# Moving work across the stage boundaries of a two-layer graph kernel: adjacency sums, scaling of h, last stores

## The chip, the cores and the metric

The kernel runs on one NeuronCore of a Trainium2 chip. The metric is the device time of one execution in microseconds (us), taken as the median of several runs. Five engines work side by side: PE (matmul), DVE (VectorE), ACT (ScalarE), POOL (GpSimd) and SP (issues DMAs). Each runs its own instructions in order.

## The reference

Two layers work on `x`, 16 batches of 1024 nodes with 256 channels, all in float32, with an adjacency matrix `adj` of 1024x1024.

- Layer 0: a graph gate (column means, sigmoid of differences, product with `adj`) gives queries, `x @ kv_w` gives keys and values, four heads of attention follow, and `x1 = layernorm(x + attention)`.
- Layer 1: `A_hat` is `adj + I`, scaled by the inverse roots of its degrees on both sides. Then

```
agg = A_hat @ x1                      # per batch
h   = relu(batchnorm(agg @ W1.T + b1))   # statistics over all batches and nodes, 512 channels
o   = batchnorm(h @ W2.T + b2)           # again over all batches and nodes, 256 channels
out = layernorm(x1 + o)
```

Each batch norm needs its statistics over all 16 batches before any of its outputs can be scaled, so it cuts the kernel into stages.

## The kernel before, in words

`fast_path` does the work (a second path is taken only when the softmax denominators leave a safe range). It has four stages. In all of them the order of the instructions on PE, ACT and DVE is the order in which the Python code issues them (`tc.manual_schedule`). The order on POOL and SP is chosen by the framework's scheduler. The framework also adds all waits: a tile's buffer is reused when its readers are done, and a pool of tiles that is laid over a closed pool waits for all of that pool's readers.

1. **Attention** (batches 0 to 15, `scores` L895 and `outputs` L911, in bursts of two units). The hooks `normalise` (L940: denominators into a PSUM tile, copy, DMAs to turn them), `residual` (L964: transposes of the outputs into PSUM, multiplication on DVE, addition to x on POOL) and `finish_x1` (L981: layer norm with eight `bn_stats` and eight scalings on DVE, then the store of x1 to DRAM on POOL's queue) are due some bursts after their group. In the last batch the adjacency is transposed, gets its degrees and is scaled: `scale_adjacency(m)` (L1070, one DVE instruction for each of eight row blocks `aht[m]`).
   After the last burst (L1197 to L1207), the aggregation of batch 0 runs as plain matmuls over m (`aggregate_first`, L1092) into two PSUM tiles of 1024 columns (`tile_s`), with one `scale_adjacency` ahead of each m. The last `normalise` and the last two `residual` stand at m=1 and m=4. Two ACT copies of 1024 columns take the sums out. Then follow on DVE the 16 additions of `adjacency_sums` (L1075) and the last `finish_x1`.
2. **Aggregation and first linear** (L1233 to L1411). Batches 1 to 15 use seven products in place of eight (`products`, L604: p1, p6, p2, p7, p5, p4, p3), of sums made beforehand: `x1_sums` on POOL for each batch, `adjacency_sums` once, `right_sums` (tile tT, DVE) for the linear. The aggregation of batch b and the linear of batch b−1 alternate on PE: after each of the seven aggregation steps `run_linear(lin, 2)` runs two linear steps (L1371 to L1375). Each step's product is added or copied by DVE or ACT, in turn on three PSUM banks a, b and c; a product that accumulates on a bank waits until the step before has read it. The h of each batch goes to DRAM. The last batch's linear (L1393 to L1411) is plain, with the batch norm's coefficients (`coefficients1`: one `bn_aggr` on DVE, five small POOL instructions) behind each of four k.
3. **Second linear** (L1420 to L1476). h is loaded in pieces of 2 MB into pool `hl` (two buffers), scaled by ACT (`scale_shift1`, L1386, four activations per batch) one batch ahead, and multiplied (L1457): for each of two output blocks c, four k and two halves. DVE takes the result out (L1468) and makes its statistics (L1472). `o2p` holds the output of all 16 batches. `hl` is opened after it.
4. **Residual and layer norm** (L1483 to L1588). `scale_shift` on ACT, transposes on PE with x1 added, statistics on DVE, ten small POOL instructions for the coefficients (among them a power, L1556), then `finish` (L1561): two blocks of 256 columns on DVE, six on ACT, and one store of 1 MB on SP's queue. x1 is loaded into `xp` (three buffers) and pool `fin2` (four).

Of the kernel before, what the change touches and what calls it, by code (L numbers as in the profile page):

```python
# [515 lines left out]
def fast_path(  # L516
# [74 lines left out]
    def layernorm(t, name):  # L591
# [7 lines left out]
        for n in range(NCH):  # L599
            nc.vector.tensor_scalar(  # L600
                t[:, n, :], t[:, n, :], mv[:, n, 0:1], rstd[:, n : n + 1], ALU.subtract, ALU.mult
            )

    def products(name, bank, out, mm, temps, bias):  # L604

# [94 lines left out]
    with (  # L700
# [391 lines left out]
        def aggregate_first(m):  # L1092
            if m == 0:
                agg[0] = xTp.tile([P, CC, N], F32, tag="xT", name="agg_0")
                agg["ps"] = [tile_s(f"pagg_{c}") for c in range(CC)]
            for c in range(CC):
                for hs in (H0, H1):
                    nc.tensor.matmul(
                        agg["ps"][c][:, hs], x1l[0][:, m, c * P : (c + 1) * P], aht[m][:, hs],
                        start=(m == 0), stop=(m == NCH - 1),  # L1100
                    )
            if m == NCH - 1:
                for c in range(CC):
                    nc.scalar.copy(agg[0][:, c, :], agg["ps"][c])

# [10 lines left out]
        with tc.manual_schedule(engines={mybir.EngineType.PE, mybir.EngineType.Activation, mybir.EngineType.DVE}):  # L1116
# [116 lines left out]
    with (  # L1233
# [126 lines left out]
        for b in range(1, B):  # L1360
            if b + 1 < B:
                load_x1l(b + 1)
                x1_sums(b + 1)
            else:
                h0 = []
# [27 lines left out]
        for k in range(HC):  # L1393
            ps = [bank(f"ph_{k}_{half}") for half in range(2)]
            for c in range(CC):
                for half, hs in enumerate((H0, H1)):
                    nc.tensor.matmul(  # L1397
                        ps[half], w1T[:, c, k * P : (k + 1) * P], t[:, c, hs],
                        start=(c == 0), stop=(c == CC - 1),
                    )  # L1400
            if k == HC - 1:
                scale_shift1(h0[0], 0)
            for half, hs in enumerate((H0, H1)):
# [4 lines left out]
            coefficients1(k)  # L1408
        for k in range(1, HC):
            scale_shift1(h0[k], k)  # L1410
# [8 lines left out]

    with tc.tile_pool(name="o2p", bufs=1) as o2p:  # L1420
        o2T = [
# [9 lines left out]
        coefficients2, sg2, sh2 = batchnorm(bn2_st, cols["g2"], cols["be2"], CC, "bn2")  # L1431
        with (
            tc.tile_pool(name="hl", bufs=2) as hl,
            tc.manual_schedule(
                engines={mybir.EngineType.PE, mybir.EngineType.Activation, mybir.EngineType.DVE}
            ),
        ):
# [8 lines left out]
            for b in range(B):  # L1446
                if b + 2 < B:
                    load_h(b + 2)
                if b + 1 < B:
                    for k in range(HC):  # L1450
                        scale_shift1(hs_of[b + 1][k], k)
                h = hs_of.pop(b)
                for c in range(CC):
                    ps = tile_s(f"po2_{b}_{c}")
                    for k in range(HC):
                        for hs in (H0, H1):
                            nc.tensor.matmul(  # L1457
                                ps[:, hs], w2T[:, k, c * P : (c + 1) * P], h[k][:, hs],
                                start=(k == 0), stop=(k == HC - 1),
                            )  # L1460
                    if b == B - 1 and c == CC - 1:
                        for hs in (H0, H1):
# [21 lines left out]
        with (  # L1484
            tc.tile_pool(name="fin2", bufs=4) as fin2,
            tc.tile_pool(name="ps_held", bufs=3, space=PSUM) as ps_held,
# [4 lines left out]
        ):  # L1491
            for b in range(3, 7):
                load_x1(b, fin2, "xf")

# [18 lines left out]

            def residual2(b):
                xt = xf[b]
# [39 lines left out]
                pool.tensor_tensor(var, var, dif, ALU.add)  # L1555
                pool.tensor_tensor(rstd, var, mhalf, ALU.pow)  # L1556
                pool.tensor_tensor(nmr, nmr, rstd, ALU.mult)
# [3 lines left out]
            def finish(b, rstd, nmr):  # L1561
                xt, hx = xf.pop(b), held.pop(b)
                y = o2T[b].rearrange("p c n -> p (c n)").rearrange("p (n c) -> p n c", c=C)
                for n in (0, 1):
                    nc.vector.tensor_scalar(
                        y[:, n, :], xt[:, n, :], rstd[:, n : n + 1], nmr[:, n : n + 1],
                        ALU.mult, ALU.add,
                    )
                for n in (4, 5, 6, 7, 2, 3):
                    nc.scalar.activation(  # L1570
                        y[:, n, :], hx[:, (n - 4) * C : (n - 3) * C] if n >= 4 else xt[:, n, :],
                        AF.Identity, bias=nmr[:, n : n + 1], scale=rstd[:, n : n + 1],
                    )
                nc.sync.dma_start(out[b].rearrange("(n p) c -> p n c", p=P), y)
                if b + 7 < B:
                    load_x1(b + 7, *((fin2, "xf") if 3 <= b < 7 else (xp, "x")))

# [4 lines left out]
            for b in range(B):  # L1582
                coeffs[b] = residual2(b)
                if b + 1 < B:
                    scale_shift(b + 1)
                if b:
                    finish(b - 1, *coeffs.pop(b - 1))
            finish(B - 1, *coeffs.pop(B - 1))  # L1588


# [41 lines left out]
```

## Time and profile before

| | us |
|---|---|
| median of 3 runs | 2637.98 (2637.81 to 2638.22) |
| the profiled execution's own time | 2637.64 |
| its span, first to last instruction | 2635.9 |
| its mean granted PE clock | 0.996 |
| stage boundary 1 to 2 | near 1708 to 1800 |
| stage boundary 2 to 3 | near 2294 to 2330 |
| last instruction that computes, its end | 2628.7 |

The profile gives for each engine the time in which it was busy, and ahead of each instruction the idle time with what ended it ("<-"). A 128x512 float32 matmul appears as two records. The end of a matmul is modelled, so the distance from start to start is the safer measure. A line number names the line of the kernel. Names are those of the program's tiles: `a_agg`, `b_agg`, `c_agg` the three banks of the aggregation's products, `a_h`, `b_h`, `c_h` those of the linear, `po` the second linear, `hl` loaded h, `hw` written h, `u_h` a temporary of the linear.

### The profile page before, as it was taken

What the parts mean: (1) busy time and instruction counts of PE and PEld (TensorE: products, weight loads), DVE (VectorE), ACT (ScalarE), POOL (GpSimd) and SP (SyncE); (2) the same over time, 40 slices, a digit from 0 to 9 for tenths busy, and PEclk for the clock granted to TensorE, in tenths of its full rate; (3) what the DMA queues carried; (4) which work ended last, traced back from release to release, by engine and by line L of the source; (5) the groups of instructions that cost most, each with busy time, mean ns of one, the idle gap of its engine ahead of it and who ended that gap; (6) DMA issues with size and microseconds to landing.
All of it is one profiled execution on the core that took longest, in us unless ns stands there. A gap on an engine that the chain in (4) does not pass through costs nothing. (4 is left out here: it accounts for less than half of the span.)

```text
span 2635.9 us, 32325 instructions
## 1 busy us (share of the span) xinstructions
PE 2572.7 (98%) x13158; PEld 1118.6 (42%) x13158; DVE 1587.8 (60%) x2159; ACT 1110.2 (42%) x1321; POOL 338.9 (13%) x407
## 2 busy tenths in 40 slices
PE   8999999999999999999999999999999999999986
PEld 4443444444434444444344443334444444444455
DVE  5465665756656657566566576766565565533367
ACT  5363563644635636546356364501100111133358
POOL 0001000100000001001000010232221122000036
PEclk9999999999999999999999999999999999999999
DMA  4001101011011010110110110112222222254458
GB/s 144 2 9 41 33 10 41 17 25 33 9 41 33 10 41 19 23 33 9 41 33 9 41 49 2 41 55 89 96 76 84 86 90 96 96 201 150 159 194 303
DMA packets 134557, 168.96 MB, mean 64 GB/s; under 512 B 86784, under 2 KB 120064, under 8 KB 124032
## 3 DMA queue, kind: packets, MB, share of 16 engines
q1 hardware_dynamic: 129568, 116.47, 14.1%
q0 software_dynamic: 4832, 50.34, 4.6%
q8 instruction: 105, 1.72, 0.3%
q14 instruction: 52, 0.43, 0.0%
HBM read 99.36 MB, written 67.44 MB: 63 GB/s over the span
## 5 line engine op out<-in xcount | busy, mean ns | idle before, releaser
L908 ACT ACTIVATE p<-ps 128x1024 f32<-128x1024 f32 x512 | 495.6, 1020 | 179.7 <-PE ps L903 132.6
L933 DVE TENSOR_TENSOR acc<-acc,p 128x1024 f32<-128x1024 f32 x384 | 483.2, 1258 | 60.9 <-ACT p L908 32.3
L903 PE MATMUL ps<-qT,kT 64*64 64x512 f32 x4096 | 490.5, 594 | 1.4 <-ACT p L908 1.4
L924 PE MATMUL po<-p,v 64*64 64x512 f32 x4096 | 485.3, 589 | 0.0
L805 PE MATMUL pg<-wg,x 128*128 128x512 f32 x960 | 425.2, 596 | 0.0
L979 POOL TENSOR_TENSOR x<-x,o 128x512 f32<-128x512 f32 x64 | 109.5, 1711 | 1434.8 <-DVE o L974 1434.8
L924 PEld LDWEIGHTS po<-p,v 64*64 64x64 f32 x4096 | 156.7, 133 | 282.8 <-issue 282.6
L805 PEld LDWEIGHTS pg<-wg,x 128*128 128x128 f32 x960 | 177.6, 190 | 226.9 <-issue 203.3
L903 PEld LDWEIGHTS ps<-qT,kT 64*64 64x64 f32 x4096 | 146.1, 132 | 280.2 <-issue 231.5
L817 ACT ACTIVATE qT<-qT 128x512 f32<-128x512 f32 x64 | 40.1, 630 | 481.9 <-DVE qT L814 481.9
L1457 PE MATMUL po<-hl,w12T 128*128 128x512 f32 x512 | 222.0, 596 | 3.6 <-ACT hl L1387 2.8
L814 DVE SCALAR_TENSOR_TENSOR qT<-pg,para_s 128x512 f32<-128x512 f32 x64 | 43.9, 689 | 270.7 <-PE pg L805 269.8
L793 DVE SCALAR_TENSOR_TENSOR wg<-wg,adj_s 128x1024 f32<-128x1024 f32 x128 | 153.1, 1217 | 16.0 <-ACT wg L789 16.0
L1457 PEld LDWEIGHTS po<-hl,w12T 128*128 128x128 f32 x512 | 97.7, 191 | 127.9 <-issue 120.4
L784 ACT ACTIVATE wg<-crow,ccol 128x1024 f32<-128x1024 f32 x128 | 146.6, 1146 | 12.2 <-DMA crow<-c 12.2
L789 ACT ACTIVATE wg<-wg 128x1024 f32<-128x1024 f32 x128 | 135.5, 1059 | 2.6
L1387 ACT ACTIVATE hl<-hl,bn_sh,bn_sg 128x1024 f32<-128x1024 f32 x64 | 74.4, 1229 | 137.4 <-DMA hl<-h 136.1
L855 PE MATMUL pv<-kvw_s,xT 128*128 128x256 f32 x512 | 124.0, 385 | 1.6 <-ACT kT L846 1.6
L1468 DVE TENSOR_SCALAR o<-po,col_b 128x1024 f32<-128x1024 f32 x31 | 39.8, 1283 | 138.1 <-PE po L1457 138.1
L842 PE MATMUL pk<-xT,kvw_s 128*128 128x512 f32 x256 | 120.3, 592 | 0.0
L855 PEld LDWEIGHTS pv<-kvw_s,xT 128*128 128x128 f32 x512 | 94.9, 190 | 51.9 <-issue 27.6
L1286 PE MATMUL b_agg<-aT,x1S 128*128 128x512 f32 x240 | 109.2, 598 | 0.0
(159 smaller groups left out, 2641.4 us busy)
## 6 DMA issues: line engine op xcount, KB each, us to landing
h<-hw POOLq DMA_DIRECT2D x16, 2048.0 KB, 6.6
hl<-h SPq DMA_DIRECT2D x15, 2048.0 KB
x<-x POOLq DMA_DIRECT2D x16, 1024.0 KB, 4.2
x1l<-x SPq DMA_DIRECT2D x16, 1024.0 KB
xf<-x SPq DMA_DIRECT2D x16, 1024.0 KB
out_dram<-o SPq DMA_DIRECT2D x16, 1024.0 KB
x<-in_x_dram SPq DMA_DIRECT2D x15, 1024.0 KB
crow<-c SPq DMA_DIRECT2D x15, 512.0 KB
```

What stands on the lines that cost most here:

```text
L784: nc.scalar.activation(w, s["crow"], AF.Abs, bias=s["ccol"][:, n : n + 1])
L789: nc.scalar.activation(w, w, AF.Tanh, scale=0.5)
L793: nc.vector.scalar_tensor_tensor(w, w, 1.0, adj_s[:, n, :], op0=ALU.subtract, op1=ALU.mult)
L805: nc.tensor.matmul(ps, xt[:, n, c * P : (c + 1) * P], s["wg", n][:, hs], start=(n == 0), stop=(n == NCH - 1),)
L842: nc.tensor.matmul(ps, kvw_s[:, c, kc * P : (kc + 1) * P], s["xT"][:, c, hs], start=(c == 0), stop=(c == CC - 1),)
L855: nc.tensor.matmul(pt[:, j * C : (j + 1) * C], s["xT"][:, c, n * P : (n + 1) * P], kvw_s[:, c, C : 2 * C], start=(c == 0), stop=(c == CC - 1),
L903: nc.tensor.matmul(ps[kh * D : (kh + 1) * D, hd * HALF : (hd + 1) * HALF], kT[r, pr, ks], qT[r, pr, qh * HALF : (qh + 1) * HALF], start=Tr ...
L908: nc.scalar.activation(p, ps, AF.Exp)
L924: nc.tensor.matmul(g["po"][kh][hd * D : (hd + 1) * D, :], s["v"][r, m, h * D : (h + 1) * D], p[r, hd * HALF : (hd + 1) * HALF], start=(m = ...
L933: nc.vector.tensor_add(g["acc"], g["acc"], p)
L979: nc.gpsimd.tensor_tensor(xs, xs, o.rearrange("p n h d -> p n (h d)"), ALU.add)
L1457: nc.tensor.matmul(ps[:, hs], w2T[:, k, c * P : (c + 1) * P], h[k][:, hs], start=(k == 0), stop=(k == HC - 1),)
```

## The change

It has these parts:

- **PSUM of the first boundary.** The sums of `aggregate_first` go to four tiles of 512 columns (the two `tile_o` and the two `tile_t`), in the order c = 1, 0, with four copies of 512 columns. The last `den` and the last two `poT` use `tile_s`.
- **Order of DVE there.** All seven remaining `scale_adjacency` stand ahead of m = 0, the `adjacency_sums` at m = 1 to 4, ahead of the last residuals. `finish_x1(15)` becomes `layernorm_steps`: statistics on DVE (and two more small POOL instructions) at the end of the loop, the scaling as eight ACT activations behind the first aggregation step of batch 1, followed by the store of x1, the load of `x1l(2)` and `x1_sums(2)`. In batch 1 the linear's steps start one aggregation step later and come in threes at i = 3 and 5.
- **Last linear of stage 2.** The halves are the outer loop of the matmuls. `scale_shift1(h0[k-2])` stands behind `coefficients1(k)`.
- **Stage 3.** Pool `hl` is opened ahead of `o2p` and lives on through stage 4. Batch 0 does k = 0, 1 for both c, then k = 2, 3. The last block of batch 15 does one half after the other. Both PSUM tiles of a batch are declared ahead of its matmuls.
- **Stage 4.** x1 of batches 3 to 6 and 10 to 13 is loaded in pairs into the buffers of `hl`; `fin2` is gone. For the last batch, the small coefficient instructions move from POOL to DVE (the power stays), `finish(14)` stands ahead of them, DVE does four blocks and ACT four, and the store is split into two halves, one on SP's queue and one on ACT's.

```diff
+    def layernorm_steps(t, name):
...
+        def statistics():
+            for n in range(NCH):
+                nc.vector.bn_stats(st[:, n, :], t[:, n, :])
+                nc.vector.bn_aggr(mv[:, n, :], st[:, n, :])
+            rsqrt(rstd, mv[:, :, 1], EPS)
+            nc.gpsimd.tensor_tensor(nmr, mv[:, :, 0], rstd, ALU.mult)
+            nc.gpsimd.tensor_scalar(nmr, nmr, -1.0, None, ALU.mult)
+
+        def apply():
+            for n in range(NCH):
+                nc.scalar.activation(
+                    t[:, n, :], t[:, n, :], AF.Identity,
+                    bias=nmr[:, n : n + 1], scale=rstd[:, n : n + 1],
+                )
...
-            den = tile_t(f"den_{k}")
+            last = k == B * PAIRS - 1
+            den = tile_s("den_last")[:, H0] if last else tile_t(f"den_{k}")
...
-            pt = tile_t(f"poT_{k}")
+            if (b, pr) == (B - 1, PAIRS - 1):
+                pt = tile_s(f"poT_{k}")[:, H0]
+            else:
+                pt = tile_t(f"poT_{k}")
...
-                agg["ps"] = [tile_s(f"pagg_{c}") for c in range(CC)]
-            for c in range(CC):
-                for hs in (H0, H1):
+                agg["ps"] = [[tile(f"pagg_{i}") for i in range(2)] for tile in (tile_o, tile_t)]
+            for c in (1, 0):
+                for half, hs in enumerate((H0, H1)):
...
             if m == NCH - 1:
-                for c in range(CC):
-                    nc.scalar.copy(agg[0][:, c, :], agg["ps"][c])
+                for c in (1, 0):
+                    for half, hs in enumerate((H0, H1)):
+                        nc.scalar.copy(agg[0][:, c, hs], agg["ps"][c][half])
...
             for m in range(NCH):
-                if m + 1 < NCH:
-                    scale_adjacency(m + 1)
+                if m == 0:
+                    for k in range(1, NCH):
+                        scale_adjacency(k)
+                elif m < 4:
+                    adjacency_sums(m - 1)
+                elif m == 4:
+                    adjacency_sums(3)
                 aggregate_first(m)
                 run(sums.get(j + m - 1, []), 9)
                 run(full.get(j + m, []), 9)
-            for i in range(NCH // 2):
-                adjacency_sums(i)
-            run(late.get(j + 5, []), 9)
+            x_last = st.pop(B - 1)["x"]
+            last_statistics, last_apply = layernorm_steps(x_last, f"l0_{B - 1}")
+            last_statistics()
...
-                run_linear(lin, 2)
+                if b > 1 or i > 0:
+                    run_linear(lin, 3 if b == 1 and i in (3, 5) else 2)
+                if b == 1 and i == 0:
+                    last_apply()
+                    nc.gpsimd.dma_start(x1_d[B - 1], x_last)
+                    load_x1l(2)
+                    x1_sums(2)
...
-            for c in range(CC):
-                for half, hs in enumerate((H0, H1)):
+            for half, hs in enumerate((H0, H1)):
+                for c in range(CC):
...
-            if k == HC - 1:
-                scale_shift1(h0[0], 0)
...
             coefficients1(k)
-        for k in range(1, HC):
+            if k > 1:
+                scale_shift1(h0[k - 2], k - 2)
+        for k in range(2, HC):
             scale_shift1(h0[k], k)
...
-    with tc.tile_pool(name="o2p", bufs=1) as o2p:
+    with tc.tile_pool(name="hl", bufs=2) as hl, tc.tile_pool(name="o2p", bufs=1) as o2p:
...
+                pss = [tile_s(f"po2_{b}_{c}") for c in range(CC)]
...
+                if b == 0:
+                    for ks in (range(HC // 2), range(HC // 2, HC)):
+                        for c in range(CC):
+                            for k in ks:
+                                for hs in (H0, H1):
+                                    mm(c, k, hs)
...
+                    if b:
+                        for k, hs in (
+                            [(k, hs) for hs in (H0, H1) for k in range(HC)] if last
+                            else [(k, hs) for k in range(HC) for hs in (H0, H1)]
+                        ):
+                            mm(c, k, hs)
...
-            for b in range(3, 7):
-                load_x1(b, fin2, "xf")
...
+            load_x1_pair(3)
+            load_x1_pair(5)
...
+                if b == B - 1:
+                    between()
...
-                pool = nc.gpsimd
+                pool = nc.vector if b == B - 1 else nc.gpsimd
...
-                pool.tensor_tensor(rstd, var, mhalf, ALU.pow)
+                nc.gpsimd.tensor_tensor(rstd, var, mhalf, ALU.pow)
...
-                for n in (0, 1):
+                last = b == B - 1
+                for n in (0, 1, 2, 3) if last else (0, 1):
...
-                for n in (4, 5, 6, 7, 2, 3):
+                for n in (4, 5, 6, 7) if last else (4, 5, 6, 7, 2, 3):
...
+                if last:
+                    nc.sync.dma_start(dst[:, M0, :], y[:, M0, :])
+                    nc.scalar.dma_start(dst[:, M1, :], y[:, M1, :])
+                else:
+                    nc.sync.dma_start(dst, y)
+                if b in (4, 6):
+                    load_x1_pair(b + 6)
```

More of the change, by code (lines that the diff above doesn't have):

```diff
@@ L602, in layernorm @@
             )
+    def layernorm_steps(t, name):
+        st = small.tile([P, NCH, 6], F32, tag="ln_st", name=f"st_{name}")
+        mv = small.tile([P, NCH, 2], F32, tag="ln_mv", name=f"mv_{name}")
+        rstd = small.tile([P, NCH], F32, tag="ln_rs", name=f"rs_{name}")
+        nmr = small.tile([P, NCH], F32, tag="ccol", name=f"nm_{name}")
+        def statistics():
[11 more added lines that the diff above has]
+                )
+        return statistics, apply
     def products(name, bank, out, mm, temps, bias):
@@ L1094, in aggregate_first @@
                 agg[0] = xTp.tile([P, CC, N], F32, tag="xT", name="agg_0")
-                agg["ps"] = [tile_s(f"pagg_{c}") for c in range(CC)]
-            for c in range(CC):
-                for hs in (H0, H1):
+                agg["ps"] = [[tile(f"pagg_{i}") for i in range(2)] for tile in (tile_o, tile_t)]
+            for c in (1, 0):
+                for half, hs in enumerate((H0, H1)):
                     nc.tensor.matmul(
-                        agg["ps"][c][:, hs], x1l[0][:, m, c * P : (c + 1) * P], aht[m][:, hs],
+                        agg["ps"][c][half], x1l[0][:, m, c * P : (c + 1) * P], aht[m][:, hs],
                         start=(m == 0), stop=(m == NCH - 1),
@@ L1360, in fast_path @@
         for b in range(1, B):
-            if b + 1 < B:
+            if 1 < b < B - 1:
                 load_x1l(b + 1)
                 x1_sums(b + 1)
-            else:
+            elif b == B - 1:
                 h0 = []
@@ L1431, in fast_path @@
         coefficients2, sg2, sh2 = batchnorm(bn2_st, cols["g2"], cols["be2"], CC, "bn2")
[L1432 to L1436, printed above, removed]
+        with tc.manual_schedule(
+            engines={mybir.EngineType.PE, mybir.EngineType.Activation, mybir.EngineType.DVE}
         ):
@@ L1452, in fast_path, with mm @@
                 h = hs_of.pop(b)
-                for c in range(CC):
[L1454 to L1461, printed above, removed]
+                pss = [tile_s(f"po2_{b}_{c}") for c in range(CC)]
+                def mm(c, k, hs):
+                    nc.tensor.matmul(
+                        pss[c][:, hs], w2T[:, k, c * P : (c + 1) * P], h[k][:, hs],
+                        start=(k == 0), stop=(k == HC - 1),
+                    )
+                if b == 0:
[4 more added lines that the diff above has]
+                                    mm(c, k, hs)
+                for c in range(CC):
+                    ps = pss[c]
+                    last = b == B - 1 and c == CC - 1
+                    if b:
[5 more added lines that the diff above has]
+                    if last:
                         for hs in (H0, H1):
@@ L1484, in fast_path @@
         with (
-            tc.tile_pool(name="fin2", bufs=4) as fin2,
             tc.tile_pool(name="ps_held", bufs=3, space=PSUM) as ps_held,
@@ L1491, in fast_path, with load_x1_pair @@
         ):
-            for b in range(3, 7):
-                load_x1(b, fin2, "xf")
+            pairs = {}
+            def load_x1_pair(b):
+                pairs[b] = hl.tile([P, 2, NCH, C], F32, tag="hl", name=f"xf_{b}_{b + 1}")
+                for i in range(2):
+                    xf[b + i] = pairs[b][:, i]
+                    nc.sync.dma_start(xf[b + i], x1_d[b + i])
+            load_x1_pair(3)
+            load_x1_pair(5)
             def scale_shift(b):
@@ L1512, in add_x1, with residual2 @@
                 )
-            def residual2(b):
+            def residual2(b, between):
                 xt = xf[b]
@@ L1573, in finish @@
                     )
-                nc.sync.dma_start(out[b].rearrange("(n p) c -> p n c", p=P), y)
-                if b + 7 < B:
-                    load_x1(b + 7, *((fin2, "xf") if 3 <= b < 7 else (xp, "x")))
+                dst = out[b].rearrange("(n p) c -> p n c", p=P)
+                if last:
+                    nc.sync.dma_start(dst[:, M0, :], y[:, M0, :])
[4 more added lines that the diff above has]
+                    load_x1_pair(b + 6)
+                elif b + 7 < B and not 3 <= b < 7:
+                    load_x1(b + 7, xp, "x")
             add_x1(0, 2)
@@ L1582, in fast_path, with before @@
             for b in range(B):
-                coeffs[b] = residual2(b)
+                def before(b=b):
+                    if b:
+                        finish(b - 1, *coeffs.pop(b - 1))
+                coeffs[b] = residual2(b, before)
                 if b + 1 < B:
                     scale_shift(b + 1)
-                if b:
-                    finish(b - 1, *coeffs.pop(b - 1))
+                    before()
             finish(B - 1, *coeffs.pop(B - 1))
```

## The prediction

> **What bounds the kernel now.** I first read the page's busy times, then PE's list of waits, then timeline and clock around each wait, and last the chain at the end.
>
> ```profile
> PE 2572.7 (98%) x13158; PEld 1118.6 (42%) x13158; DVE 1587.8 (60%) x2159; ACT 1110.2 (42%) x1321; POOL 338.9 (13%) x407
> ```
>
> PE is 98% busy, and the diff removes no matmul. A gain can only come from PE's 63 us of idle time, from time in which PE ran slowly, and from the tail after PE's last matmul. The waits of PE that lie where the diff edits:
>
> ```profile
> PE b_h L1318 <- DVE u_h L615: 3.4, 2, 1.9
> PE po L1457 <- ACT hl L1387: 2.8, 1, 2.8
> PE b_h L1318 <- DVE tT L667: 1.8, 1, 1.8
> PE a_agg L1286 <- ACT agg L1104: 1.1, 1, 1.1
> ```
>
> (total us, times, longest.) PE's timeline at the first boundary, attention to aggregation:
>
> ```profile
> 1741.21 3.70 PE L1286 MATMUL a_agg<-ahT,x1l 128*128 128x512 f32 x8 [1.10 <-ACT agg L1104]
> 1744.75 1.02 PE L1318 MATMUL a_h<-agg,w12T 128*128 128x512 f32 x2
> 1747.54 1.10 PE L1318 MATMUL b_h<-tT,wS 128*128 128x512 f32 x2 [1.77 <-DVE tT L667]
> ...
> 1757.06 1.02 PE L1318 MATMUL c_h<-tT,wS 128*128 128x512 f32 x2
> 1759.95 1.57 PE L1318 MATMUL b_h<-tT,w12T 128*128 128x512 f32 x2 [1.88 <-DVE u_h L615]
> 1761.31 4.90 PE L1286 MATMUL b_agg<-aT,x1S 128*128 128x512 f32 x8
> 1766.05 1.02 PE L1318 MATMUL c_h<-agg,wS 128*128 128x512 f32 x2
> ```
>
> Undisturbed, two records take 0.86 us from start to start and eight take 3.43. At 1761.31 eight take 4.74: the granted clock halves after the 1.88 us wait. (Columns: window and length, busy us of PE, PEld, DVE, ACT and POOL, granted clock, DMA share, GB/s.)
>
> ```profile
> 1761.00:1762.00 1.00, 1.00 (x2) 0.34 (x1) 0.44 (x1) 0.00 (x0) 0.00 (x0) 0.50 1.04 434
> 2328.00:2329.00 1.00, 1.00 (x2) 0.34 (x1) 0.00 (x0) 1.00 (x2) 0.00 (x0) 0.50 0.97 401
> ```
>
> The second line is the other boundary, first linear to second. The chain of waits there:
>
> ```profile
> 2309.47 6.63 DMA h<-hw
> ...
> 2316.25 8.34 DMA hl<-h
> ...
> 2324.69 1.25 ACT hl L1387
> ```
>
> The load of h(1) starts only when the last store of h has landed; then its scaling, then PE.
>
> **First boundary.** Costs by starts of PE instructions, in the profiled execution:
> - ahT wait: m=5 starts at 1729.15, m=6 could at 1732.58, starts at 1732.97: 0.39. All scalings now go first on DVE: seven from 1711.29 at about 2.0 each beside POOL (10.12 for five), done near 1725. PE takes 3.43 per m. This goes.
> - a_agg: 16 records from 1732.97 would let it start at 1739.83; it starts at 1741.21: 1.38. The eight-bank pool takes over PSUM only after every reader of the old one. The last copy becomes 128x512 (0.58, row of L623) in place of 128x1024 (1.01): 0.43 goes, 0.95 stays.
> - b_h at 1747.54 could start at 1745.61: 1.93 goes, if tT is there in time.
> - b_h at 1759.95 could start at 1757.92: 2.03 goes. u_h stood behind eight normalisations (L600, 2.67) on DVE, which move to ACT.
> - The half clock behind it: (1761.31−1759.95−0.86)+(4.74−3.43) = 1.81.
>
> Sum 6.6; less 0.1 where three products run in a row (p3 needs the add of p5: 0.69 and hand-overs against 0.86 of cover): **6.5**.
>
> Do the moved steps fit? DVE from 1711.29: scalings 13.5, the 16 adjacency sums 0.605 each = 9.7 (now ahead of the residuals), the two residuals 3.1 with POOL's addition between, statistics 8x0.53 = 4.2: done near 1742.3; tT 4x0.6, so tT[1] near 1743.5. PE: p1 of aggregation from 1740.4, p6 from 1743.8, first linear step at 1747.3, first use of tT[1] at 1748.1. Cover 4.6 us; at the slow 1.67 per addition that tT has beside POOL (1783.61) 2.5 remain. In m=0 the last product waits for the oT addition that reads its bank (ends 1711.37, free otherwise at 1710.8); the 1.34 us wait for ahT at 1713.27 swallows that.
>
> New wait: eight activations (L1570: 1.93 for four, so 4.0) stand on ACT behind the p1 copy and wait for POOL (0.24+1.66+two small, near 1744.8). Behind them stands the p_h copy: ready 1748.3, starts 1748.8. DVE's u_h addition waits for it, and PE for that only at p7, 1753.3. Cost nothing, cover nearly 4 us. On POOL the x_15 store is issued (0.63) after the activations and x1_sums(2) (4x1.7) follow, to 1756; needed near 1780. SP's load of x1l_2 waits for x1l_0 as before. The 1.51 us wait of b=2 (1794.33) has its cause (tT beside POOL, the range check) unchanged and stays.
>
> **Second boundary.** PE's 32 records from 2309.14 end their pitch at 2322.86; b=1 starts at 2325.99: 3.13. Half clock after it: (1−0.56)+0.5+0.5+(1−0.73) = 1.71 over four 1-us windows. Counting pool sizes per partition, the h buffers lay over the store buffers of the stage before (hp); opened ahead of o2p they lie over crp and wgp, whose last reader is PE near 2292.9. Then two loads of 2 MB go at 2293 beside the store of h(14) (2295.9): 6 MB at 420 GB/s are there by 2308. ACT does h0 as before (to 2313.9), then h(1) 4x1.16 to 2318.6, before 2322.86. Price: o2p now lies over hp, so DVE's first eviction waits for the store of h(15) (lands 2316.1). Splitting b=0 by k moves that eviction from 2316.4 to 2319.7: 3.6 us cover, so nothing. If nothing hid it, the late store is the next bound. The order of halves in the last linear and of scaling and copies leaves ACT's row as it was: nothing. **4.8**.
>
> [...]
>
> **End.** The last output in halves: ACT's first copy and bn_stats (1.29 for two) are done while PE works, 0.6 gained. x1 loads in pairs: no PE wait names them before; the first pair comes earlier, pairs 10 and 12 one batch (5 us) later, about 20 us ahead of use: nothing. The last batch:
>
> ```profile
> 2623.49 1.68 POOL w_l L1556
> ...
> 2626.71 1.99 ACT o L1570 x4
> ```
>
> The small operations on DVE (0.2 each, row L1056) start behind finish(14) (0.72), so 2622.16+7x0.2+0.1+1.68+0.1+2x0.2 = 2625.8: as late as POOL now. Then ACT has four activations, not six: end 2627.75 for 2628.69; DVE's half ends 2627.3. The last 1 MB store is issued at 2628.72, its packets run from 2629.6 to 2633. A first half issued at 2627.35 and a second on ACT's queue 0.45 later end near 2631.6: 1.35. ACT's queue has no row; SP's issue takes 0.39, and a whole us more would still be hidden by the first half's 1.5 us. [...] But queued transfers of this stage ran at 404 GB/s in 2580 to 2600 with a DMA share of 1.05 [...]; I keep 1.35. **1.95**.
>
> **Sum.** 6.5+4.8+1.95 = 13.3. Profiled execution: span 2635.9, own time 2637.64, giving 2624.3; the median is 0.34 higher: **2624.7**.
>
> **Rivals.**
> - A: POOL takes x1_sums(2) ahead of the statistics' coefficients. Before, POOL did just that (1744.96 against 1754.54); now the statistics are 12 us earlier and x1l_2 lands no sooner than 1744.5, which speaks against. Sums to 1751.9, coefficients 1754.6, activations 1758.6, p_h 1759.2, while PE stops at 1752.4: 6.8 plus 1.7 clock: 2633.2. 7%.
> - B: the h loads still wait for the old stage's stores. The second boundary gives nothing: 2629.5. 9%.
> - C: the waits at the first boundary only move on, since DVE's work stays the same and is merely sorted: half of it comes back: 2628. 4%. DVE's 60% speaks against.
> - D: slower. Both PSUM tiles of the second linear are now declared before its first matmul. If a bank is taken at declaration, each batch's first matmul waits for the last eviction (L1468 1.28, plus 0.3). It decides if that wait comes in all 15 batches: +23.7, 2648. The pagg tiles were declared in pairs too and no such wait shows there, but both were free. 4%.
> - E: more goes, for instance the 1.51 wait with its 0.16 of drain and a faster tail: 2622. 12%.
> - The forecast, 2621 to 2628: 64%.
>
> **The numbers.** 2620 to 2631 takes in the forecast, B, C and E and leaves out A, D and the edges, under 2 in 10. A measurement of this kernel tells 0.2% (5.3 us) from no change. Faster 0.90 (all but most of A and D), same 0.06, slower 0.04.
>
> **What would show it.** Step by step: a_agg's wait down to about 0.7 and no wait on tT or u_h before 1770; PEclk 1.00 there and at the second boundary; hl loads issued near 2293 and no PE wait on ACT hl; b=0's eviction not waiting for a DMA; bn_mv 0.6 sooner behind PE's last po; two stores at the end, ACT's last activation about 3 us before the packets stop. Wrong, if ACT shows a wait on POOL of several us near 1750, or po a wait on DVE each batch.

## The result, and the profile after

| | us |
|---|---|
| before, median of 22 runs beside the changed kernel | 2637.41 (2633.08 to 2638.22) |
| changed, median of 22 runs | 2632.18 (2630.65 to 2633.03) |
| ratio changed / before | 0.9982, 95% interval 0.9976 to 0.9988 |
| changed, profiled execution: own time, span | 2632.21, 2630.1 |

The change gains 5.2 us where 13.3 were forecast; 2632.18 lies above the range of 2620 to 2631. Runs of one kernel can fall into two groups a few us apart (before: most near 2637.5, a few near 2633.5 at a mean granted clock 0.001 higher; below, e6_warm: 10 of 21 near 2628, 11 near 2634; e3_second and e4_end too), so profiled executions are compared by stage, not by their totals.

PE's busy time stays (2571.8, before 2572.7). Of the four waits shown of before, tT and h(1) are gone from the list, u_h has 1.5 left and a_agg 0.7. One has grown from 0.78, that for the copies of the first linear (total us, times, longest):

```profile
PE po L1494 <- ACT hw L1443: 4.7, 1, 4.7
```

PE's timeline at the first boundary:

```profile
1740.30 3.70 PE L1321 MATMUL a_agg<-ahT,x1l 128*128 128x512 f32 x8 [0.68 <-ACT agg L1134]
...
1759.38 1.13 PE L1353 MATMUL c_h<-agg,wS 128*128 128x512 f32 x2
...
1776.65 3.60 PE L1321 MATMUL a_agg<-ahT,x1l 128*128 128x512 f32 x8
...
1787.76 1.12 PE L1353 MATMUL b_h<-tT,wS 128*128 128x512 f32 x2 [1.51 <-DVE u_h L640]
```

No wait and no slow stretch from 1741 to 1786 (clock 1.00). p1 (the first product) of batch 2 starts at 1776.65; before it was later:

```profile
1783.21 3.60 PE L1286 MATMUL a_agg<-ahT,x1l 128*128 128x512 f32 x8
```

The second boundary, before: PE's first matmul of the second linear, and on ACT the last copy, which waits for PE alone, with two scalings of h(0) behind it:

```profile
2309.14 14.00 PE L1457 MATMUL po<-hl,w12T 128*128 128x512 f32 x32 [0.78 <-ACT hw L1404]
```

```profile
2308.39 0.69 ACT L1404 ACTIVATE hw<-ph,col_b 128x512 f32<-128x512 f32 x1 [0.17 <-PE ph L1397]
2308.98 2.36 ACT L1387 ACTIVATE hl<-hl,bn_sh,bn_sg 128x1024 f32<-128x1024 f32 x2
```

Changed: first PE, then ACT, then the clock at three places (columns as in the prediction):

```profile
2287.90 13.90 PE L1438 MATMUL ph<-agg,w12T 128*128 128x512 f32 x32
2306.53 23.85 PE L1494 MATMUL po<-hl,w12T 128*128 128x512 f32 x51 [4.73 <-ACT hw L1443]
```

```profile
2297.20 1.24 ACT L1428 ACTIVATE hl<-hl,bn_sh,bn_sg 128x1024 f32<-128x1024 f32 x1 [1.55 <-DMA hl<-h]
...
2299.25 1.24 ACT L1428 ACTIVATE hl<-hl,bn_sh,bn_sg 128x1024 f32<-128x1024 f32 x1 [0.24 <-POOL bn_sh L1264]
2300.40 0.67 ACT L1443 ACTIVATE hw<-ph,col_b 128x512 f32<-128x512 f32 x1
...
2304.66 1.24 ACT L1428 ACTIVATE hl<-hl,bn_sh,bn_sg 128x1024 f32<-128x1024 f32 x1 [1.89 <-POOL bn_sh L1264]
2305.81 0.67 ACT L1443 ACTIVATE hw<-ph,col_b 128x512 f32<-128x512 f32 x1
```

```profile
1761.00:1762.00 1.00, 1.00 (x3) 0.38 (x2) 1.00 (x3) 0.00 (x0) 0.00 (x0) 1.00 0.00 0
2307.00:2308.00 1.00, 1.00 (x2) 0.34 (x1) 0.97 (x2) 1.00 (x2) 0.43 (x1) 0.50 0.08 33
2536.00:2537.00 1.00, 1.00 (x6) 1.00 (x6) 0.96 (x3) 1.00 (x2) 0.00 (x0) 0.50 0.05 16
```

Between the copies of the last first-linear (hw) stand scalings of h(1) (hl). The first waits for its load, the other two shown for POOL's coefficients, and the copies behind them wait along. The coefficients in turn need the copies ahead of them: POOL starts the third set at 2302.94, in e1_fix below, where no scaling of h(1) stands between, at 2300.95. The last copy starts at 2305.81, though PE's matmuls end near 2301.8. The clock is full at the first boundary, but half behind the new wait, and half a third time at the start of the last stage (2536), where it was full before.

All profiled executions, cut at three starts: the last first-linear (ph), the first addition of x1 (held, the start of the last stage), and ACT's part of the last finish. The first column is the median of a kernel's runs, the others are of its one profiled execution. The last column names the boundaries at which a half clock lies (1: first, 2: second, 4: start of the last stage; one at the kernel's start and one run of them after PE's last work are in all).

| kernel | median | to ph | ph to held | held to last finish | to the span's end | half clock |
|---|---|---|---|---|---|---|
| before | 2637.4 | 2294.46 | 240.84 | 90.49 | 10.07 | 1, 2 |
| changed | 2632.2 | 2287.90 | 241.68 | 91.64 | 8.86 | 2, 4 |
| e1_fix | 2627.2 | 2287.89 | 236.03 | 91.28 | 9.36 | 4 |
| e2_first | 2631.6 | 2288.13 | 240.63 | 90.58 | 10.02 | 2 |
| e3_second | 2640.4 | 2294.47 | 241.68 | 91.91 | 10.35 | 1, 2, 4 |
| e4_end | 2635.2 | 2295.48 | 238.83 | 91.63 | 8.46 | 1, 4 |
| e5_banks | 2625.8 | 2287.51 | 235.45 | 91.18 | 9.42 | 4 |
| e6_warm | 2633.6 | 2288.89 | 236.03 | 91.85 | 9.43 | none |
| e7_behind | 2633.3 | 2287.99 | 243.68 | 90.12 | 8.79 | 2 (twice as long) |
| e8_all | 2627.4 | 2288.58 | 235.45 | 91.87 | 9.43 | none |
| e9_warm2 | 2625.0 | 2288.12 | 235.45 | 90.09 | 9.46 | none |
| e10_shift | 2626.6 | 2288.52 | 236.89 | 90.18 | 9.45 | none |
| e11_sp | 2624.0 | 2287.00 | 235.45 | 90.10 | 9.02 | none |

Changed against before: 6.56 − 0.84 − 1.15 + 1.21 = 5.78 of span; outside the span 0.35 more is spent, for a reason that no profile shows, which leaves 5.43 between the two profiled executions.

### The profile page after: what moved, and what is told of

It is laid out like the page before. It is cut to its first block, busy times and chain, and to the rows that moved or that the text cites. A ratio compares the mean times of both kernels' runs of the same rounds, so it can differ in the third digit from the quotient of the medians.

```text
span 2630.1 us, 32333 instructions
## 1 busy us (share of the span) xinstructions
PE 2571.8 (98%) x13158; PEld 1119.8 (43%) x13158; DVE 1585.7 (60%) x2162; ACT 1113.6 (42%) x1329; POOL 335.8 (13%) x400
## 4 chain that ended last, share of the span: by engine, by line
PE 87%; DVE 7%; ACT 4%; issue 1%; DMA 1%; POOL 0%; POOLq 0%; DVEq 0%; ACTq 0%
PE ps L928 17%; PE po L949 16%; PE pg L830 16%; PE po L1494 8%; PE pv L880 4%; PE b_agg L1321 4%; PE pk L867 4%; PE c_agg L1321 4%; PE a_agg L1321 2%; PE b_h L1353 2%; PE c_h L1353 2%; ACT o L1635 1%; PE den L972 1%; ACT o L1561 1%; PE a_h L1353 1%
## 5 line engine op out<-in xcount | busy, mean ns | idle before, releaser
L1321 PE MATMUL a_agg<-ahT,x1l 128*128 128x512 f32 x240 | 108.1, 593 | 0.7 <-ACT agg L1134 0.7
```

Source lines behind the costliest of these rows:

```text
L1321: nc.tensor.matmul(ps, left, right, start=(start and i == 0), stop=(i == NCH // 2 - 1), skip_group_check=True,)
```

## The experiments

**e1_fix: h(1) held behind h(0).** The changed kernel, and:

```diff
-                    for k in range(HC):
-                        scale_shift1(hs_of[b + 1][k], k)
+                    with tc.issue_after(h0_done.ins) if b == 0 else ExitStack():
+                        for k in range(HC):
+                            scale_shift1(hs_of[b + 1][k], k)
...
```

(h0_done is the last scaling of h(0), ahead in the source; the edge orders the issue on ACT alone.)

> The changed kernel, with one edge added: the four scalings of h(1) on ACT stand behind the last scaling of h(0), as they did in the kernel before. Theory (order on ACT): in the changed kernel the last two copies of b = 15's first linear stood behind three scalings of h(1), which waited 1.55 for the load and 0.24 and 1.89 for POOL's coefficients. Without them the last copy starts some 3.9 us earlier, PE's wait ahead of po of b = 0 falls from 4.73 to about 0.8 (before: 0.78), the half clock that followed it (1.7) goes too: 2632.2 - 3.9 - 1.7 = 2626.6 us, 2625.5 to 2628. Rival 1 (the copies are late because of the early loads of h(1) or of POOL's coefficients, whatever ACT's order): the wait stays above 3 us and the time within 1 us of 2632. Rival 2 (the wait moves on): the copies are early, but po then waits as long for a scaling of h(0) or h(1): 2629.5 to 2632.

Measured: 2627.16 (2626.68 to 2627.76), ratio to before 0.9962 (0.9949 to 0.9976). PE, then ACT, then the clock:

```profile
2287.89 13.90 PE L1438 MATMUL ph<-agg,w12T 128*128 128x512 f32 x32
2302.56 47.90 PE L1495 MATMUL po<-hl,w12T 128*128 128x512 f32 x111 [0.78 <-ACT hw L1443]
```

```profile
2301.82 0.69 ACT L1443 ACTIVATE hw<-ph,col_b 128x512 f32<-128x512 f32 x1 [1.03 <-PE ph L1438]
2302.41 2.36 ACT L1428 ACTIVATE hl<-hl,bn_sh,bn_sg 128x1024 f32<-128x1024 f32 x2
```

```profile
2303.00:2304.00 1.00, 1.00 (x4) 0.42 (x3) 0.97 (x2) 1.00 (x2) 0.57 (x1) 1.00 0.70 295
```

The wait is 0.78 again, no wait for h(1) follows, and the clock behind it is full. From ph to held it takes 236.03, before 240.84: 4.81 gained, where the forecast said 4.8. The loads of h(1) are issued as early as in the changed kernel (2286.37, there 2286.38); only ACT's order was edited. Both rivals fall. A half clock at the start of the last stage remains.

**e2_first, e3_second, e4_end: one part each, on the kernel before.** Their cores:

```diff
 e2_first
+                agg["ps"] = [[tile(f"pagg_{i}") for i in range(2)] for tile in (tile_o, tile_t)]
...
+            last_statistics()
...
+                    last_apply()
+                    nc.gpsimd.dma_start(x1_d[B - 1], x_last)
+                    load_x1l(2)
+                    x1_sums(2)
 e3_second
+            if k > 1:
+                scale_shift1(h0[k - 2], k - 2)
...
+    with tc.tile_pool(name="hl", bufs=2) as hl, tc.tile_pool(name="o2p", bufs=1) as o2p:
...
+                    for ks in (range(HC // 2), range(HC // 2, HC)):
 e4_end
+                            [(k, hs) for hs in (H0, H1) for k in range(HC)] if last
...
+                pool = nc.vector if b == B - 1 else nc.gpsimd
...
+                    nc.sync.dma_start(dst[:, M0, :], y[:, M0, :])
+                    nc.scalar.dma_start(dst[:, M1, :], y[:, M1, :])
```

> The kernel before with the first boundary's part of the change alone (PSUM tiles of the first aggregate, order of the adjacency sums, b = 15's layer norm on ACT in two steps, loads and sums of b = 2 later). Theory: 6.5 us, as the traces of the two kernels differ there (1783.21 to 1776.65): 2637.4 - 6.5 = 2630.9, 2630.3 to 2632.5 (the upper end if the start of the last stage falls into a half clock, as in the changed kernel). Rival (part of the gain at that place was the load order of the later parts, or is given back behind it): 2632.5 to 2636.

Measured: 2631.63 (2630.70 to 2632.59), ratio 0.9978 (0.9969 to 0.9987). To ph 2288.13, 6.3 less than before; the stages behind it as before. The first part gains its 6 us alone and gives nothing back.

> The kernel before with the second boundary's part alone (pool of h opened ahead, so that h(1) loads early; half-by-half order of the last first-linear; scalings of h(0) behind the copies; order of po for b = 0; loads of x1 in pairs). Theory: the early loads let three scalings of h(1) in among the copies on ACT, so PE waits 4 to 5 us ahead of po of b = 0 in place of 0.78 there and 3.13 later: slower than before or the same, 2637.4 + 0.8 = 2638.2, 2637 to 2640. The recorded forecast, for itself: 2637.4 - 4.8 = 2632.6. Rival (the loss comes only together with the other parts): 2632 to 2634.

Measured: 2640.39 (2636.75 to 2641.59), ratio 1.0013 (1.0006 to 1.0020): this part alone makes the kernel slower. PE waits:

```profile
PE po L1453 <- ACT hw L1402: 4.7, 1, 4.7
```

The wait of 4.7 comes with this part and nothing else; ph to held takes 241.68, as in the changed kernel. Theory said 2638.2; a half clock at the start of the last stage came on top (held to last finish 91.91 for 90.49).

> The kernel before with the end's part alone (half order of the last po block; batch 15's small operations on DVE, four parts of its finish on each of DVE and ACT, store in two parts on two queues, finish of b = 14 ahead of the small operations). Theory: nothing from the half order (the one PSUM tile of two banks has a single wait, so that ACT still starts behind the last matmul, 0.5 us or so), 2.1 from the last statistics to the last byte, up to 0.9 given back behind it: 2637.4 - 1.7 = 2635.7, 2635.2 to 2636.6. Recorded forecast: 1.95, of which 0.6 by the half order: 2635.4, with ACT's first half starting about 1.7 us ahead of the last matmul's end. Rival (the start of the last stage falls into a half clock because of the new order): 2637 to 2638.

Measured: 2635.21 (2630.91 to 2636.48), ratio 0.9989 (0.9983 to 0.9996). PE waits 1.36 for ACT's copies of the last block, as before, so the half order gives nothing. In its profile the half clock has moved from the second boundary, whose code is untouched, to the start of the last stage. PE's wait for h(1), then the clock behind it, then the clock at the start of the last stage:

```profile
2326.69 23.87 PE L1456 MATMUL po<-hl,w12T 128*128 128x512 f32 x55 [2.54 <-ACT hl L1387]
```

```profile
2327.00:2328.00 1.00, 1.00 (x3) 0.38 (x2) 0.00 (x0) 1.00 (x2) 0.00 (x0) 1.00 0.95 410
2541.00:2542.00 1.00, 1.00 (x6) 1.00 (x6) 0.96 (x3) 1.00 (x2) 0.00 (x0) 0.50 1.02 426
```

The wait for h(1) was 2.54 here and 2.85 before, yet no half clock followed; at the start of the last stage the gaps are those of before (1.36, 2.32), yet half clock followed. The grid, in the last section, sorts these cases. The three parts add up: −5.9 + 2.8 − 2.4 = −5.5 of medians, for −5.2 measured together, though the half clocks of the parts and of the whole do not lie at the same places.

**e7_behind: the pool of h back behind the outputs.** The changed kernel, and:

```diff
-    with tc.tile_pool(name="hl", bufs=2) as hl, tc.tile_pool(name="o2p", bufs=1) as o2p:
+    with tc.tile_pool(name="o2p", bufs=1) as o2p, tc.tile_pool(name="hl", bufs=2) as hl:
```

> The changed kernel with one thing undone: the pool of h is opened behind that of the outputs again, so that the load of h(1) waits for the last stores of h as before. Theory (the early h(1) let its scalings in among the copies): ACT has the four scalings of h(1) behind those of h(0) again; po of b = 0 waits 0.78 for the copy instead of 4.73, and 2.5 to 3.1 for h(1) come back ahead of po of b = 1. Net 0.8 to 1.5 less than the changed kernel, and up to 1.7 either way by where the half clock falls: 2630.6, 2629.3 to 2632.3. Rival (the scalings stood among the copies because of the new order of copies and scalings of h(0) in the source): the wait of 4.73 stays, and 3 more come: 2635.

Measured: 2633.28 (2631.77 to 2633.92), ratio 0.9989 (0.9981 to 0.9998), above the expected range. PE, then SP:

```profile
2302.67 14.00 PE L1494 MATMUL po<-hl,w12T 128*128 128x512 f32 x32 [0.78 <-ACT hw L1443]
2320.98 29.52 PE L1494 MATMUL po<-hl,w12T 128*128 128x512 f32 x61 [4.31 <-ACT hl L1428]
```

```profile
2309.87 0.32 SPq L1470 DMA_DIRECT2D xf<-x  x1
2310.49 0.79 SPq L1480 DMA_DIRECT2D hl<-h  x2
```

The theory on the order holds: with h(1) late, ACT has its scalings behind those of h(0) and po of b = 0 waits 0.78 for the copies. The size was missed: the wait for h(1) is 4.31, not 2.5 to 3.1. A 1 MB load of x1 is now issued 0.6 ahead of h on SP's queue; counted from ph, h is issued 0.7 later than before, and takes 9.09 to land for 8.34. That the load of x1 causes both was not tested. The half clock lasts two stretches (2320.37 to 2327.20).

**e5_banks: the last block in two PSUM tiles.** e1_fix, and:

```diff
-                pss = [tile_s(f"po2_{b}_{c}") for c in range(CC)]
+                pss = [tile_s(f"po2_{b}_{c}") for c in range(1 if b == B - 1 else CC)]
+                if b == B - 1:
+                    pss.append([tile_t("po2_last_0"), tile_t("po2_last_1")])
...
```

> e1_fix, with the last output block of b = 15 in two PSUM tiles of one bank each instead of one tile of two banks. Theory (one tile, one wait): in the changed kernel and in e1_fix ACT's first copy of that block starts only behind the last matmul, though the first half's matmuls end four instructions (1.7 us) earlier. With two tiles ACT's first half starts about 1.7 us sooner, so only one bn_stats (0.65) instead of two stands between the last matmul and the coefficients: 2627.2 - 0.6 = 2626.6, 2626.0 to 2627.2. Rival (ACT waited for something else, or the coefficients wait elsewhere): the start of stage 4 stays where it is, 2627.2. The granted clock at the start of the last stage is to be read beside it: if the half clock there goes because of the shift, up to 1.7 more.

Measured: 2625.77 (2624.85 to 2627.27), a little under the expected 2626.0 to 2627.2; 0.4 of the gain is that ph starts sooner (2287.51 for 2287.89), which the edit does not touch. First the changed kernel's ACT, then this kernel's:

```profile
2528.26 1.27 ACT L1517 ACTIVATE o<-po,col_b 128x512 f32<-128x512 f32 x2 [0.58 <-PE po L1494]
```

```profile
2518.79 0.69 ACT L1522 ACTIVATE o<-po_last,col_b 128x512 f32<-128x512 f32 x1 [11.51 <-PE po_last L1498]
...
2522.22 0.69 ACT L1522 ACTIVATE o<-po_last,col_b 128x512 f32<-128x512 f32 x1 [0.59 <-PE po_last L1498]
```

In one tile both halves start together behind PE's last matmul; in two the first is copied 3.43 ahead of the second (1.7 was expected). ph to held falls by 0.58 (236.03 to 235.45), as the forecast's 0.6 had it. The tile of two banks had one wait, in whatever order the matmuls wrote it.

**e6_warm, e8_all, e9_warm2: filling PE's wait at the start of the last stage.** e6_warm is e1_fix, e8_all is e5_banks, each with five more matmuls whose result is overwritten; e9_warm2 is e5_banks with two:

```diff
                     pt = ps_sum.tile([P, HALF], F32, tag="sum", name=f"pf_{b}_{pair}")
+                    for _ in range(5 if b == 0 and pair == 0 else 0):
+                        nc.tensor.matmul(
+                            pt, ident, xt[:, 4:6, :].rearrange("p n c -> p (n c)"),
+                            start=True, stop=True,
+                        )
```

> e1_fix, with five matmuls 128x512 more, whose result nobody reads (they write the PSUM tile that the first transposes of b = 0 then overwrite); they fill the 2.32 us in which PE waits for ACT's scaling at the start of the last stage. Theory (the half clock comes from PE's idle time): the clock stays 1.00 behind it, the 14 matmuls that took 2.84 to 3.36 take 1.83 again, and the time falls by about 1.5: 2625.7, 2625 to 2626.5. Rival 1 (the 1.36 us of idle time ahead of the first of them is enough, or the half clock falls there whatever PE does): clock 0.5 stays, 2627.2 or up to 1 more. Rival 2 (clock restored but ACT and DVE set the pace of this stage): clock 1.00 and 2626.9 to 2627.3.

Measured: 2633.62 (2627.48 to 2634.61), 6 above e1_fix. The profiled execution took 2628.41, so its stages do not account for that median; what made it stays open, as no profile shows it. First e1_fix, then this kernel:

```profile
2528.34 1.75 PE L1585 MATMUL pf<-ident,o 128*128 128x128 f32 x7 [2.32 <-ACT o L1562]
2529.88 2.84 PE L1600 MATMUL held<-ident,o 128*128 128x128 f32 x16
```

```profile
2526.74 4.45 PE L1583 MATMUL pf<-xf,ident 128*128 128x512 f32 x10
...
2531.90 1.95 PE L1605 MATMUL held<-ident,o 128*128 128x128 f32 x16
```

No half clock (the 16 take 1.95, in e1_fix 2.84), but one of these matmuls is two records of 0.43, so five took 4.3 us and not the 2.2 that I had reckoned. They ran 1.7 past the wait and, in the profiled execution, gave back what the clock brought.

> e1_fix with both: two PSUM tiles for the last block, and the five filling matmuls. If both theories hold: 2627.2 - 0.6 - 1.5 = 2625.1, 2624.5 to 2626. If only one of them holds, 2625.7 or 2626.6; if PE's idle time at the start of the stage isn't what the clock falls by, 2626.6.

Measured: 2627.38 (2625.91 to 2627.68), slower than e5_banks for the same reason: held to last finish 91.87 for 91.18. Expected were 2624.5 to 2626.

> e5_banks with two filling matmuls in place of e8_all's five (one of them takes 0.86 us here, so five took 4.3 and ran 1.7 to 2 past the wait of 2.3 that they were to fill; two take 1.72). Theory (a stretch of 3.413 us in which PE idles for more than about half is followed by one at half clock): PE's idle time in any one such stretch at the start of the last stage falls to 1.4 or less, no half clock, and nothing is delayed: e5_banks 2625.8 less 1.2 = 2624.6, 2624.0 to 2625.4. Rival (the stage's pace is ACT's and DVE's, the half clock there costs nothing on the path): 2625.5 to 2626.

Measured: 2624.97 (2624.46 to 2625.25), ratio 0.9953 (0.9939 to 0.9966). First the changed kernel, then this one:

```profile
2535.40 3.36 PE L1599 MATMUL held<-ident,o 128*128 128x128 f32 x14 [0.20 <-ACT o L1561]
```

```profile
2525.39 1.88 PE L1587 MATMUL pf<-xf,ident 128*128 128x512 f32 x4
...
2529.38 1.83 PE L1609 MATMUL held<-ident,o 128*128 128x128 f32 x14 [0.20 <-ACT o L1566]
```

The same 14 matmuls took 3.36 at half clock. Held to last finish is 90.09, in e5_banks 91.18: between these two the half clock cost 1.1.

**e10_shift: the same gaps, one matmul (0.86) later.** e1_fix, and:

```diff
+                    nc.tensor.matmul(
+                        pss[0][:, H0], w2T[:, 0, :P], h[0][:, H0], start=True, stop=True
+                    )
                     for ks in (range(HC // 2), range(HC // 2, HC)):
```

> e1_fix with one matmul 128x512 more ahead of the first output group of b = 0 (0.86 us; its result is overwritten), so that everything behind it comes 0.86 later with the same gaps. In the traces so far each half clock begins a whole number of times 3.4133 us after the one before it (0, 507, 673 and 760 in the kernel before), and the same gaps at the start of the last stage (1.36, 2.3) are followed by half clock in some kernels and not in others. Theory (a fixed grid of 3.413 us, half clock behind a stretch of it with more than half idle): shifted by 0.86 the 2.33 gap is cut by a boundary of the grid into about 1.5 and 0.9, no stretch has more than 1.5 us idle, and the half clock at the start of the last stage goes: 2627.2 + 0.86 - 1.2 = 2626.8, with clock 1.00 there. Rival (the length of the gaps decides): half clock there as in e1_fix, 2628.0.

Measured: 2626.64 (2625.69 to 2627.17), half a microsecond less than e1_fix with 0.86 more work (the runs of the two overlap):

```profile
2529.82 0.98 PE L1587 MATMUL pf<-ident,o 128*128 128x128 f32 x7 [2.32 <-ACT o L1564]
...
2531.23 1.83 PE L1602 MATMUL held<-ident,o 128*128 128x128 f32 x14 [0.20 <-ACT o L1564]
```

The gap is 2.32 as in e1_fix (the one of 1.36 ahead of it too), and the clock behind it full: 14 matmuls in 1.83. The length of the gaps alone doesn't decide. How far they moved against the clock's grid is in the last section.

**e11_sp: both halves of the last store on SP's queue.** e9_warm2, and:

```diff
-                    nc.scalar.dma_start(dst[:, M1, :], y[:, M1, :])
+                    nc.sync.dma_start(dst[:, M1, :], y[:, M1, :])
```

> e9_warm2 with the second half of the last store issued by SP too, behind the first half, in place of ACT's queue. In the traces the issue on ACT's queue took 0.42 to 0.43 in two kernels (the changed one, e4_end) and 1.8 to 2.0 in the others with this end; where it took long, the DMA share falls to about 0.4 for half a microsecond between the two halves and the data end some 0.7 later. SP's issue took 0.37 in all. Theory: the two halves follow without a gap, 0.6 sooner: 2625.0 - 0.6 = 2624.4, 2624.0 to 2624.8. Rival (the second half is late for another reason, or what follows the last byte makes it up): 2624.8 to 2625.3; if the two halves on one queue wait for one another, 2626.

Measured: 2624.02 (2623.63 to 2625.17), ratio 0.9951 (0.9938 to 0.9965), the fastest of all. Between the halves in e9_warm2, and here:

```profile
2617.50:2618.00 0.50, 0.00 (x0) 0.00 (x0) 0.00 (x0) 0.00 (x0) 0.00 (x0) 0.50 0.26 88
```

```profile
2615.50:2616.00 0.50, 0.00 (x0) 0.00 (x0) 0.00 (x0) 0.00 (x0) 0.00 (x0) 0.50 0.95 297
```

The hole (DMA share 0.26) is gone, and last finish to end falls from 9.46 to 9.02. That is 0.4 of the 0.95 between the medians. In the profiles ph starts 1.1 sooner here, with the same code up to there; where the clock's grid lies in an execution goes with that (last section), and the edit has no part in it.

## Why the prediction was wrong

- **First boundary, 6.5: right.** 6.56 in the changed kernel, 6.3 in e2_first. Step by step: the ahT and tT waits and the 2.03 of u_h gone, a_agg at 0.68 (about 0.7 forecast), p3 0.09 late (0.1), half clock gone, 1.51 at batch 2 unchanged. The mechanism held, not only the sum. Rival A did not happen: POOL had the coefficients ready before ACT's activations at 1745.68.
- **Second boundary, 4.8: the step that failed.** It read "The order of halves in the last linear and of scaling and copies leaves ACT's row as it was: nothing" and "ACT does h0 as before (to 2313.9), then h(1)". The loads came when forecast (issued 2286.38; the forecast's 2293 is on before's clock and less the 6.56 gained ahead of it is 2286.4; its 420 GB/s is close to the 419 that before's DMA view of 2285 to 2335 shows), and no matmul waited for the store of h(15). But I took the order on ACT to be that of the source throughout. It is kept within one `manual_schedule` block; h(1) is scaled in the next block, and once its data was due early, its scalings were placed among the copies. They wait for the load and for coefficients, and PE waits for the copies behind them: 4.73 for 0.78, then half clock. Result −0.84 in place of +4.8, which is 5.6 of the 7.9 that the profiled execution misses. e1_fix shows it from one side (+4.81 with the order held), e3_second (the wait comes with this part alone) and e7_behind (it goes when h(1) comes late) from the other.
- **Half clocks.** I counted 1.81 and 1.71 as gone with their waits. That holds while no other stretch falls to half. In the changed kernel one did, at the start of the last stage, where the code and the gaps are as before; held to last finish takes 91.64, with this end and full clock 90.1 (e7_behind, e9_warm2, e10_shift): 1.5 lost. The sum had no term for it. e9_warm2 shows that it comes from PE's idle time there, e10_shift that the length of the gaps does not settle it. That the changed kernel's profile has it and before's does not is in part where the gaps happened to fall on the grid (64% of a stretch idle for 40%, last section), so luck.
- **End, 1.95.** The 0.6 by halves did not come (one tile, one wait; 0.58 in e5_banks once it has two). Nothing from pairs, as forecast. The tail, 1.35: at full clock held to last finish is 0.39 shorter (90.1 for 90.49), and from there to the end 1.21, so 1.6 of span; the 0.35 outside the span goes off it. The split cost no rate: while the two halves of 512 KB moved, the DMA share in windows of half a us was 1.02 to 1.06 in the changed kernel (319 to 356 GB/s, 2624.0 to 2626.5) and 0.95 to 1.07 in e11_sp (297 to 369 GB/s, 2615.0 to 2618.0), where before's store of 1 MB ran at 330 to 365 GB/s (2630.0 to 2632.5).

Together: 6.56 − 0.84 − 1.54 + 1.60 − 0.35 = 5.43. Rivals B, C, D did not happen (the loads were early, nothing moved on at the first boundary, no po waits for a DVE eviction). With the two things made true that the forecast took for granted, the order held and the halves in two tiles, the kernel takes 2625.8 (e5_banks), 1.1 above the forecast of 2624.7, and 1.1 is what the half clock at the start of the last stage cost there. That e11_sp, with two filling matmuls and SP's queue besides, takes 2624.0 is no support for the forecast, which had neither.

## What to carry to other kernels

An order written out by hand holds only inside the block that writes it: when a change makes data of a later block ready early, read the instruction order on the engine that both blocks share, and pin the new work behind the old. A result needed half by half should lie in two tiles: in one, a single wait held both halves here, in two the first went 3.43 ahead of the second (e5_banks). Before booking a stretch of half clock as gained, ask what idle time of PE remains elsewhere, since moving it against the clock's grid brought a half clock to a place that had none (2536, clock 0.50). By an estimate from e9_warm2's trace (last section), filling that idle time leaves at most 23% of a stretch idle wherever the grid lies; shifting it (e10_shift) left 53% where the grid lay in its profile.

## What was not expected of the hardware

**The half clocks of an execution lie on a grid of 3.4133 us.** The kernel before, around its half clock at the first boundary:

```profile
1760.50:1761.00 0.50, 0.50 (x2) 0.30 (x1) 0.18 (x1) 0.00 (x0) 0.00 (x0) 0.51 0.64 262
...
1763.50:1764.00 0.50, 0.50 (x2) 0.12 (x1) 0.00 (x0) 0.00 (x0) 0.00 (x0) 0.58 0.12 33
```

The clock is 1.00 in the windows on both sides, so with means of 0.51 and 0.58 the half clock begins 0.01 into the first of these and ends 0.42 into the second: 1760.51 to 1763.92, 3.41 us. Half clocks of one execution begin whole multiples of 3.4133 us apart: before at 29.95, 1760.51, 2327.12, 2624.08 (507.0, 673.0 and 760.0 behind the first); changed at 29.94, 2306.63, 2535.32, 2620.66 (667.0, 734.0, 759.0); the other profiles fit to 0.02. Laid over PE's gaps, the grid sorts the cases (place: the end of the stretch):

| kernel, place | PE idle in the stretch of 3.41 | next stretch |
|---|---|---|
| changed, 2306.6 | 3.3 (97%) | half |
| e1_fix, 2528.3 | 2.3 (68%) | half |
| before, 2327.1 | 2.3 (67%) | half |
| changed, 2535.3 | 2.2 (64%) | half |
| before, 1760.5 | 1.9 (55%) | half |
| e10_shift, 2529.3 | 1.8 (53%) | full |
| e4_end, 2328.5 | 1.6 (48%) | full |
| e7_behind, 2535.4 | 1.6 (48%) | full |
| before, 2535.3 and 2538.7 | 1.4 (40%) | full |

So in these runs it is not the length of a gap that sorts the cases but its share of one stretch: a gap of 1.88 within one stretch was followed by half clock, one of 2.54 cut in two was not. In these rows full clock follows up to 53% and half clock from 55% on, and that is no sharp bound: at the kernel's start and end 53% (1.80, e5_banks up to 28.78) was followed by half and 54% (1.84, e11_sp up to 2609.04) by full. In e7_behind the half clock stayed for a second stretch in which PE had been idle for 0.61 us; where PE was busy throughout (before at 1763.92, changed at 2310.04) it ended after one.

**Where the grid lies differs between executions.** PE's first matmul starts between 4.8 and 5.1 in all 13 profiles, but the half clock at the kernel's start begins anywhere from 28.56 (e11_sp) to 31.46 (e6_warm). PE's pace at the start differs with it: in before its first eight matmul records of 128x512, from 8.50, take 4.08, where eight take 3.60 at 1783.21, and from 8 to 12 us PE, busy throughout, has 15 records in e11_sp, 14 in before and 12 in e6_warm. The later the grid, the later ph: the ten kernels with the first part reach it in the very order of their grids, from 2287.00 to 2288.89. Before and changed have the same grid (29.95 and 29.94), so their stages compare fairly. e4_end's lies 1.35 later than before's, and e10_shift's 0.98 later than e1_fix's: its gaps come 1.49 later, so against the grid they moved by 0.51, not by 0.86, and 1.8 us idle fell into one stretch where at most 1.5 was expected.

One profile thus does not tell whether a half clock belongs to a kernel. Three estimates follow from laying the gaps of one trace on the grid of another. With e1_fix's gaps on e10_shift's grid, the worst stretch would be 68% idle, so there the added matmul (53%) made the difference; with e5_banks's gaps on e9_warm2's grid it would be 67%, so there the filling did. With before's gaps about two places of the grid in three give a stretch over 54% idle at the start of the last stage; with e9_warm2's no place gives more than 23%.

**The issue of a store on ACT's queue** took 0.42 to 0.43 in the changed kernel and e4_end, and 1.76 to 2.02 in seven others with the same instruction. Why is open; SP's took 0.37 each time. It does not settle the tail by itself: with 1.76 e7_behind takes 8.79 from last finish to end, the changed kernel with 0.43 takes 8.86.
